# A pre-activation block with table lookups on one Trainium2 core: the order of loads, warm-up products and weight differences at the start of two of its layers

## The chip, the core and the metric

The kernel runs on one core of a Trainium2 chip. The metric is device microseconds of one execution; the time of a kernel is the median of its runs. A core has engines that each work off an instruction queue of their own, in order: TensorE (PE, matrix products; PEld is its weight load), VectorE (DVE), ScalarE (ACT), GpSimd (POOL) and SyncE (SP), which issues most of the transfers. An engine waits on semaphores for what other engines and transfers produce.

## The reference, cut to what matters

Everything is float32. The input has 32 images of 1024 channels, 14 x 14 positions.

```python
def _amm(patches, centroids, lut, inv_temp):       # approximate product by lookup
    v = patches.reshape(B, ncb, sub, H * W).transpose(0, 3, 1, 2)
    scores = 2.0 * einsum('blcs,cks->blck', v, centroids) - sum(centroids * centroids, -1)
    attn = softmax(scores * inv_temp, axis=-1)     # over the 16 centroids of a codebook
    out = einsum('blck,cko->blo', attn, lut)
...
out = _amm(gn(x), c1_centroids, c1_lut, c1_invt)                 # 1024 -> 256, sub 4
out = relu(_bn(out, bn1_g, bn1_b))
out = _amm(_extract3x3(out), c2_centroids, c2_lut, c2_invt)      # 3x3 patches, sub 9
out = relu(_bn(out, bn2_g, bn2_b))
out = _bn(_amm(out, c3_centroids, c3_lut, c3_invt), bn3_g, bn3_b)
x = x + relu(out + gn(x))
x = x + linear_attention_block(gn(x))
```

gn normalises each image in 32 groups of channels; _bn uses mean and variance over all images. The last line is a linear attention with rotary tables and a depthwise 3x3 product; the change doesn't touch it.

## The kernel before, in words

The kernel goes through four stages one after the other: layer 1 (the first lookup product with its group normalisation), layer 2 (the 3x3 one), layer 3, and a last stage with the attention. Each of layers 1 and 2 is worked in 128 **units**: 16 pairs of images (392 positions) by 8 tables of weights. Unit u uses pair u // 8 and table u % 8. A second pass with exact maxima is compiled too and entered only if a check on the sums asks for it; it isn't executed here.

What happens to a unit, with the engine and the lines:

- **Score**: PE multiplies the normalised images with the prepared centroids into four PSUM buffers (L910 in layer 1, L1051 in layer 2). ACT takes exponentials of them into a tile t (L576).
- **Softmax**: DVE transposes t so that the 16 centroids lie side by side (L588), POOL adds halves (L591, from unit 2 on), DVE sums (L607), takes reciprocals (L609) and transposes them back, repeated (L619, tile r), ACT adds up totals for the check (L630), POOL multiplies t by r (L626).
- **Rows**: The 16th centroid's share is one minus the rest, so its row of t is free and used to carry another sub-table's data. For that POOL writes one of every four units' slices to a spare (L621) and SP issues transfers from the spare into the free rows of t (L725, L728).
- **Lookup**: PE multiplies t with the table, 12 or 16 products (L748).

The loop `units` (L732) writes these out by hand, in this order for each i: score and exponentials of unit i + 4, transposition of i + 3, softmax and rows of i + 2 (or i + 3 for the first units), then `side(i)` (L838 in layer 1, `side2`, L1062, in layer 2), which carries whatever has been put at step i, then the lookup of unit i (units 0, 1 and 2 are looked up at i = -2, 0 and 1). Each engine's queue has its instructions in the order in which they are written, so where a piece is written decides what stands behind it. `at(i, piece)` (L806) puts a piece at step i; pieces meant for before the loop come at -5.

A table of weights has to be prepared before its lookup. `packed_lut` (L679) returns the pieces for it, by which the diff indexes: [1] **own** (L687) loads it from memory, [2] **less** (L694) takes the difference to the 16th centroid's entry, [3] **keep** (L703, tables 0 and 4 only) stores a slice to memory, [4] **others** (L706) loads rows from what was kept. A difference is, for each of two halves, one product with a constant matrix on PE (L700) and a copy on ACT (L701):

```python
def less():
    for h in range(2):
        t = weights[b][:, 512 * h : 512 * h + 512]
        ps = scores(512) if b > 3 else None
        if ps is None:
            ps = ps_po.tile([P, 512], F32, tag="po", name="less")
        nc.tensor.matmul(ps, less_last, t, start=True, stop=True)
        nc.scalar.copy(t, ps)
```

The constant matrix `less_last` is made by DVE from an identity matrix (`last_masks`, L673 to L677), with `kmask`, which is made from the identity too (`kmasks`, L215). The identity and three other constants are loaded through ACT's queue at the start (L181). `warm` (L567) multiplies by the identity without using the result.

Layer 1's start, L872 to L902: SP loads the first pair of images (`load_x`, L237), tables 0 and 1, the second pair, tables 2 to 7. DVE makes masks, centroid matrices (L346 to L392) and the statistics of the first pair (L264). The pieces of a group normalisation (`gn_pieces`, L246) are four statistics pieces on DVE, two averages over groups on PE (L274) with DVE between (L282 to L288), and a power and a product on POOL (L295, L296); ACT then normalises channel by channel (L825). For the second pair (x_1) these pieces are put at steps -3 to 2. The scores' bias is a product with a reduction (L401 to L410).

Layer 2's start, L1018 to L1040: ACT normalises the first channels of layer 1's output into a padded tile (L990, `store_pair`, L988), SP stores it to memory (L1002), and 3x3 patches are loaded from there, six transfers to a patch (`load_patches`, L1006, L1012). There are four patch buffers. With `engines=both` transfers alternate by row offset between SP and ACT. `second_half` (L1032) does the same for the other half of the channels.

The last stage isn't written out by hand: a planner (`Plan`, L51) takes pieces with engine, rank, cost and dependences and writes them by simulated due times (L83). It goes round a Python set of engines (L90, L117).

Of the kernel before, what the change touches and what calls it, by code (L numbers as in the profile page):

```python
# [20 lines left out]
HW = 196  # L21
# [128 lines left out]
def conv_preact_kernel(ctx: ExitStack, tc: tile.TileContext, a: dict, out: bass.AP):  # L150
    nc = tc.nc
# [59 lines left out]
    def masks():  # L211
        nc.vector.tensor_reduce(mask8, mask1.rearrange("p (j c) -> p c j", c=8), AX.X, ALU.add)
        nc.vector.tensor_reduce(mask4, mask1.rearrange("p (j c) -> p j c", c=8), AX.X, ALU.add)

    def kmasks():  # L215
        nc.vector.tensor_reduce(kmask, ident.rearrange("p (c k) -> p k c", k=KC), AX.X, ALU.add)
# [290 lines left out]
    def layers(exact, early=None):  # L507
# [59 lines left out]
        def warm(n, rhs):  # L567

            t = scores(rhs.shape[1])
            for _ in range(n):  # L570
                nc.tensor.matmul(t, ident, rhs, start=True, stop=True)
# [222 lines left out]
        with ExitStack() as s:  # L794
# [5 lines left out]
            AHEAD = 2 if exact else 4  # L800
# [50 lines left out]
            luts2 = [packed_lut(2, b) for b in range(8)]  # L851
# [3 lines left out]
                    at(8 * p + c - AHEAD - 1 - (p == 0), normalise(p, c))  # L855
            at(24, edges)
            at(40, masks2)
            for b, i in enumerate((-4, -4, -3, -3, -1, 1, 2, 3)):
                for k in (2, 3, 4):
                    if k != 3 or b % 4 == 0:  # L860
                        at(i, lambda b=b, k=k: luts[b][k]())
# [8 lines left out]

            luts = [packed_lut(1, b) for b in range(8)]
            xts[0] = load_x(xp, 0)  # L872
            for b in range(2):
                luts[b][1]()
            xts[1] = load_x(kept, 1)
            for b in range(2, 8):
                luts[b][1]()
            if not exact:
                masks()
            bias1, biases = score_biases(ps_tr, once, st, 1, raw[1], P, CT, mask8, 4)  # L880
            w1 = score_matrices(once, 1, "", raw[1], mask8)
            gn = [
# [89 lines left out]
        with ExitStack() as s:  # L972
# [4 lines left out]
            NPB = 4  # L977
# [50 lines left out]
            luts2[3][2]()  # L1028
            load_patches(2)
            load_patches(3)  # L1030

            def second_half():  # L1032
                for b in range(4):
                    luts2[b][4](nc.scalar)
                store_pair(0, 1)
                if not exact:
                    load_patches(NPB)

            if exact:
                second_half()  # L1040
            w9, bias2 = parts[2]

            def score2(u):
# [17 lines left out]

            def side2(i):  # L1062

                if i == 1 - ahead and not exact:
                    second_half()
# [47 lines left out]
        with ExitStack() as s:  # L1113
# [8 lines left out]
            luts = luts3  # L1122
# [1176 lines left out]
```

## Time and profile before

| | us |
|---|---|
| three runs | 3385.02, 3385.55, 3385.81; median 3385.55 |
| the profiled execution | 3385.66 |
| its span | 3383.0 |
| layer 1: first score (L910) | 20.11 |
| layer 1: lookups 0, 1, 2, 3 begin (L748) | 33.58, 43.88, 53.11, 65.59 |
| layer 1: lookups 4, 5, 6, 7 begin | 71.83, 77.31, 83.62, 90.43 |
| layer 2: first score (L1051) | 840.07 |
| layer 2: lookups 0, 1, 2, 3 begin | 855.87, 866.85, 877.71, 888.45 |
| layer 2: lookups 4, 5, 6, 7 begin | 894.79, 899.81, 906.15, 912.48 |

The last stage begins at about 2284. TensorE's granted clock over the execution was 0.994 of full speed. In the profile's rows a group is written as tile written <- tiles read, with the number of instructions; "idle before" is how long the engine had stood still and what it was released by. A queue with a q (SPq, ACTq) is an engine issuing transfers.

### The profile page before, as it was taken

What the parts mean: (1) busy time and instruction counts of PE and PEld (TensorE: products, weight loads), DVE (VectorE), ACT (ScalarE), POOL (GpSimd) and SP (SyncE); (2) the same over time, 40 slices, a digit from 0 to 9 for tenths busy, and PEclk for the clock granted to TensorE, in tenths of its full rate; (3) what the DMA queues carried; (4) which work ended last, traced back from release to release, by engine and by line L of the source; (5) the groups of instructions that cost most, each with busy time, mean ns of one, the idle gap of its engine ahead of it and who ended that gap; (6) DMA issues with size and microseconds to landing.
All of it is one profiled execution on the core that took longest, in us unless ns stands there. A gap on an engine that the chain in (4) does not pass through costs nothing. (4 is left out here: it accounts for less than half of the span.)

```text
span 3383.0 us, 61034 instructions
## 1 busy us (share of the span) xinstructions
PE 3300.1 (98%) x22287; PEld 2012.1 (59%) x22287; DVE 2872.0 (85%) x4174; ACT 1789.7 (53%) x4419; POOL 2528.3 (75%) x1562
## 2 busy tenths in 40 slices
PE   8999999999999999999999999989999999999998
PEld 4555555554445544444478888876666666666665
DVE  8999999996888898888666666655899999989996
ACT  5555555553444444444311111108888888888885
POOL 5999999996788889888532222216988888898887
PEclk9999999999999999999999999999999999999999
DMA  3110111003444344443231111113222333233221
GB/s 120 46 49 28 47 46 47 27 27 86 133 124 125 112 121 122 123 112 104 63 89 40 50 50 50 49 48 127 70 83 84 89 93 93 83 94 97 72 87 39
DMA packets 242250, 266.31 MB, mean 79 GB/s; under 512 B 32812, under 2 KB 239700, under 8 KB 241944
## 3 DMA queue, kind: packets, MB, share of 16 engines
q1 hardware_dynamic: 240400, 261.20, 26.3%
q8 instruction: 179, 2.93, 0.4%
q10 hardware_dynamic: 1544, 1.13, 0.1%
q14 instruction: 127, 1.04, 0.1%
HBM read 171.01 MB, written 75.58 MB: 73 GB/s over the span
## 5 line engine op out<-in xcount | busy, mean ns | idle before, releaser
L626 POOL TENSOR_TENSOR t<-t,r 128x1568 f32<-128x1568 f32 (+5 forms) x292 | 962.0, 3296 | 531.5 <-issue 222.8
L748 PE MATMUL po<-t,lut 128*128 128x392 f32 x3840 | 1331.1, 499 | 8.0 <-DMA t<-spare 8.0
L748 PEld LDWEIGHTS po<-t,lut 128*128 128x128 f32 x3840 | 710.1, 190 | 606.1 <-issue 83.3
L1806 PE MATMUL mm<-y,lut 128*128 128x392 f32 x2048 | 713.5, 494 | 6.1 <-ACT vt L1871 4.1
L588 DVE STREAM_TRANSPOSE tt<-t 128x1568 f32<-128x1568 f32 (+1 forms) x284 | 517.5, 1822 | 158.9 <-ACT t L576 155.9
L576 ACT ACTIVATE t<-sc,cbias 128x392 f32<-128x392 f32 (+1 forms) x624 | 322.4, 597 | 560.0 <-PE sc L910 189.6
L2030 DVE SCALAR_TENSOR_TENSOR pa<-y,lepe_w,pa 128x406 f32<-128x406 f32 x900 | 533.5, 635 | 22.2 <-PE pa L2012 20.0
L619 DVE STREAM_TRANSPOSE r<-rc 128x1568 f32<-128x1568 f32 (+1 forms) x284 | 520.8, 1834 | 11.6 <-POOL t L626 1.2
L1806 PEld LDWEIGHTS mm<-y,lut 128*128 128x128 f32 x2048 | 370.0, 188 | 249.6 <-ACT vt L1871 5.0
L591 POOL TENSOR_TENSOR tt<-tt 128x784 f32<-128x784 f32 x252 | 463.4, 1839 | 15.0 <-DVE tt L588 14.9
L576 ACT ACTIVATE t<-sc,room 128x392 f32<-128x392 f32 x512 | 259.1, 589 | 390.9 <-issue 156.8
L1388 PE MATMUL po<-t,lut 128*128 128x224 f32 (+2 forms) x1352 | 313.3, 414 | 0.0
L607 DVE TENSOR_REDUCE sm<-tt 128x98 f32<-128x784 f32 (+2 forms) x284 | 297.0, 1046 | 1.2 <-POOL tt L591 0.8
L1388 PEld LDWEIGHTS po<-t,lut 128*128 128x128 f32 (+1 forms) x1352 | 233.4, 189 | 62.9 <-issue 60.6
L609 DVE RECIPROCAL rc<-sm 128x98 f32<-128x98 f32 (+1 forms) x284 | 220.1, 775 | 9.8
L630 ACT ACTIVATE sm<-sm 128x98 f32<-128x98 f32 (+1 forms) x284 | 85.2, 300 | 154.5 <-DVE rc L609 154.5
L1659 ACT ACTIVATE w<-x,tb,gn_a 128x196 f32<-128x196 f32 x248 | 128.3, 517 | 39.9 <-POOL y L1541 28.1
L1992 POOL TENSOR_TENSOR qr<-qr,zb 128x784 f32<-128x784 f32 x64 | 118.1, 1855 | 28.6 <-DMA zb<-zd 25.7
L1818 ACT ACTIVATE e<-e 128x392 f32<-128x392 f32 x256 | 134.4, 525 | 1.4
L1772 ACT ACTIVATE y<-x,gb,ga 128x196 f32<-128x196 f32 x256 | 122.8, 542 | 14.4 <-POOL gb L1735 14.2
L825 ACT ACTIVATE x<-x,gn_b,gn_a 128x196 f32<-128x196 f32 x256 | 127.5, 557 | 4.8 <-POOL gn_b L296 4.3
L1401 DVE TENSOR_TENSOR o<-po,o 128x224 f32<-128x224 f32 (+1 forms) x156 | 81.5, 543 | 56.8 <-PE po L1388 51.9
(215 smaller groups left out, 4516.7 us busy)
## 6 DMA issues: line engine op xcount, KB each, us to landing
patch<-h1d SPq DMA_DIRECT2D x382, 108.5 KB
x<-in_x_dram SPq DMA_DIRECT2D x32, 784.0 KB
o3d<-o SPq DMA_DIRECT2D x56, 448.0 KB
x<-in_x_dram SPq DMA_DIRECT2D x64, 392.0 KB
out_dram<-x SPq DMA_DIRECT2D x64, 392.0 KB
o<-o3d SPq DMA_DIRECT2D x62, 392.0 KB
h1d<-pad SPq DMA_DIRECT2D x96, 225.0 KB
patch<-h1d SPq DMA_DIRECT2D x382, 54.2 KB
```

Source lines behind the costliest of these rows:

```text
L576: nc.scalar.activation(t[:, j, : sc.shape[1]], sc, AF.Identity if exact else AF.Exp, bias=bias[:, j : j + 1],)
L588: nc.vector.transpose(tt, tf)
L591: nc.gpsimd.tensor_tensor(tv[:, :, :8], tv[:, :, :8], tv[:, :, 8:], ALU.add)
L607: nc.vector.tensor_reduce(sm, tv, AX.X, ALU.add)
L609: nc.vector.reciprocal(rc, sm)
L619: nc.vector.transpose(r, bc(rc, 2, KC))
L626: nc.gpsimd.tensor_tensor(v[:, c], v[:, c], r[:, c], ALU.mult)
L748: nc.tensor.matmul(po[h], luts[b][:, j, h * P : (h + 1) * P], ts[u % len(ts)][:, j, :N2], start=(b == 0 and j == j0), stop=(b == 7 and j = ...
L1388: nc.tensor.matmul(dst, w, x, start=start, stop=stop)
L1806: nc.tensor.matmul(pv(), w[kt][:, m0 : m0 + P], ywin(p, first + kt), start=(kt == 0), stop=(kt == 3),)
L1818: nc.scalar.activation(e(), e(), AF.Exp, scale=-1.0)
L2030: nc.vector.scalar_tensor_tensor(acc, neighbours(p, c, offset(k)), lw[:, c, k : k + 1], acc, ALU.mult, ALU.add,)
```

## The change

In layer 1:

- SP loads all eight tables before the second pair of images.
- `kmasks` and `last_masks` are written before the bias and the centroid matrices, where kmasks was behind the statistics and last_masks behind the bias.
- The warm-up of 9 products has 4, the second warm-up (4 products) is gone.
- The differences of tables 0 and 1 stand behind the warm-up, that of table 2 behind the bias product. Tables 3 and 4 follow the first score, 5 and 6 the second, 7 the third (before: 0 and 1, 2 and 3 behind the first two scores, then 4 at i = -1 and 5, 6, 7 at 1, 2, 3).
- The pieces of x_1's normalisation stand at -1, -1, 0, 0, 1, 1, 2, 2, 2 in place of -3, -3, -2, -1, 0, 0, 1, 1, 2.

In layer 2:

- ACT issues its share of patch 0 alone (by row offsets 2 of its 6 transfers). Patch 1's share, the load of table 7 (4 transfers) and the rows of tables 0 to 3 are issued by SP.
- Before the loop only tables 0 and 1 have their difference; 2, 3 and 4 come at i = -4, -3, -1 and 5, 6, 7 at 4, 5, 6 (before: 0 to 3 before the loop, 4 to 7 at -3, -1, 1, 2).
- The rows (others) of table 0 stand behind patch 3, of 1 at -3, of 2 and 3 at -2, of 4 at 1, of 5, 6, 7 at 4, 5, 6 together with the difference. The load of table 7 stands at -1.

The diff, without what concerns the exact pass alone:

```diff
@@ layer 1 @@
-            for b, i in enumerate((-4, -4, -3, -3, -1, 1, 2, 3)):
+            for b, i in ((3, -4), (4, -4), (5, -3), (6, -3), (7, -2)):
                 for k in (2, 3, 4):
                     if k != 3 or b % 4 == 0:
                         at(i, lambda b=b, k=k: luts[b][k]())
...
             xts[0] = load_x(xp, 0)
-            for b in range(2):
+            for b in range(8):
                 luts[b][1]()
             xts[1] = load_x(kept, 1)
-            for b in range(2, 8):
-                luts[b][1]()
             if not exact:
                 masks()
+                kmasks()
+            last_masks()
             bias1, biases = score_biases(ps_tr, once, st, 1, raw[1], P, CT, mask8, 4)
             w1 = score_matrices(once, 1, "", raw[1], mask8)
...
-            warm(9, xts[0][:, 0, :HW])
-            for k, f in enumerate(gn[0]):
+            warm(4, xts[0][:, 0, :HW])
+            luts[0][2]()
+            luts[0][3]()
+            luts[1][2]()
+            for f in gn[0]:
                 f()
-                if k == 3 and not exact:
-                    kmasks()
             ts = unit_tiles(AHEAD + 2)
             biases()
-            last_masks()
-            warm(4, xts[0][:, 1, :HW])
+            luts[2][2]()
+            for b in range(3):
+                luts[b][4]()
...
             for k, f in enumerate(gn[1]):
-                at((-3, -3, -2, -1, 0, 0, 1, 1, 2)[k] if AHEAD > 2 else k - 7, f)
+                at((-1, -1, 0, 0, 1, 1, 2, 2, 2)[k] if AHEAD > 2 else k - 7, f)
@@ layer 2 @@
-            both = nc.sync, nc.scalar
             store_pair(0, 0)
             luts2[0][2]()
+            load_patches(0, engines=(nc.sync, nc.scalar))
             luts2[1][2]()
-            load_patches(0, engines=both)
-            load_patches(1, engines=both)
-            luts2[7][1](nc.scalar)
+            load_patches(1)
             luts2[0][3]()
-            luts2[2][2]()
-            luts2[3][2]()
             load_patches(2)
             load_patches(3)
+            luts2[0][4]()

             def second_half():
-                for b in range(4):
-                    luts2[b][4](nc.scalar)
+                luts2[1][4]()
                 store_pair(0, 1)
-                if not exact:
-                    load_patches(NPB)
+                load_patches(NPB)
...
             def side2(i):
-                if i == 1 - ahead and not exact:
-                    second_half()
-                if i == 2 - ahead and not exact:
-                    load_patches(NPB + 1)
-                for b in range(4, 8):
-                    if i == (max(b - 7, -ahead) if exact else (-3, -1, 1, 2)[b - 4]):
-                        luts2[b][2]()
-                    if i == max(b - 4, 0):
-                        luts2[b][4]()
-                if i == max(-2, -ahead):
-                    luts2[4][3]()
+                if exact:
+                    ...
+                else:
+                    if i == -3:
+                        second_half()
+                    if i == -2:
+                        luts2[2][4]()
+                        luts2[3][4]()
+                        load_patches(NPB + 1)
+                    if i == -1:
+                        luts2[7][1]()
+                    b = {-4: 2, -3: 3, -1: 4, 4: 5, 5: 6, 6: 7}.get(i, 0)
+                    if b:
                         luts2[b][2]()
+                    if b == 4:
+                        luts2[b][3]()
+                    if b > 4 or i == 1:
+                        luts2[b or 4][4]()
```

More of the change, by code (lines that the diff above doesn't have):

```diff
@@ L1017, in load_patches @@
                         )
-            both = nc.sync, nc.scalar
             store_pair(0, 0)
             luts2[0][2]()
+            load_patches(0, engines=(nc.sync, nc.scalar))
             luts2[1][2]()
-            load_patches(0, engines=both)
-            load_patches(1, engines=both)
-            luts2[7][1](nc.scalar)
+            load_patches(1)
             luts2[0][3]()
-            luts2[2][2]()
-            luts2[3][2]()
             load_patches(2)
             load_patches(3)
+            luts2[0][4]()
             def second_half():
-                for b in range(4):
-                    luts2[b][4](nc.scalar)
+                luts2[1][4]()
                 store_pair(0, 1)
-                if not exact:
-                    load_patches(NPB)
+                load_patches(NPB)
             if exact:
-                second_half()
+                for b in (2, 3):
+                    luts2[b][2]()
+                    luts2[b][4]()
+                luts2[1][4]()
+                luts2[7][1]()
+                store_pair(0, 1)
             w9, bias2 = parts[2]
@@ L1062, in side2 @@
             def side2(i):
-                if i == 1 - ahead and not exact:
-                    second_half()
-                if i == 2 - ahead and not exact:
-                    load_patches(NPB + 1)
-                for b in range(4, 8):
-                    if i == (max(b - 7, -ahead) if exact else (-3, -1, 1, 2)[b - 4]):
+                if exact:
+                    for b in range(4, 8):
+                        if i == max(b - 7, -ahead):
+                            luts2[b][2]()
+                        if i == max(b - 4, 0):
+                            luts2[b][4]()
+                    if i == max(-2, -ahead):
+                        luts2[4][3]()
+                else:
[6 more added lines that the diff above has]
+                    if i == -1:
+                        luts2[7][1]()
+                    b = {-4: 2, -3: 3, -1: 4, 4: 5, 5: 6, 6: 7}.get(i, 0)
+                    if b:
                         luts2[b][2]()
-                    if i == max(b - 4, 0):
-                        luts2[b][4]()
-                if i == max(-2, -ahead):
-                    luts2[4][3]()
+                    if b == 4:
+                        luts2[b][3]()
+                    if b > 4 or i == 1:
+                        luts2[b or 4][4]()
                 p = {4: 1}.get(i + ahead, (i + ahead + 9) / 8)
```

## The prediction

> **What bounds the kernel now.** I read the share of busy time first, then busy time in stretches of 20 us, then the timeline of the two places that the change touches.
>
> The page's engine line:
>
> ```profile
> PE 3300.1 (98%) x22287; PEld 2012.1 (59%) x22287; DVE 2872.0 (85%) x4174; ACT 1789.7 (53%) x4419; POOL 2528.3 (75%) x1562
> ```
>
> TensorE is busy for 98% of the span: little beyond the two starts can be gained. Stretches (columns: length, busy PE, weight load, DVE, ACT, POOL, granted clock, DMA share, GB/s):
>
> ```profile
> 0.00:20.00 20.00, 8.17 (x36) 7.10 (x36) 11.05 (x42) 2.27 (x3) 2.28 (x9) 1.00 0.92 276
> 20.00:40.00 20.00, 16.53 (x64) 6.73 (x63) 17.80 (x26) 15.62 (x35) 8.19 (x7) 1.00 0.38 122
> 40.00:60.00 20.00, 18.84 (x71) 9.29 (x70) 19.23 (x29) 10.25 (x25) 15.76 (x8) 1.00 0.33 97
> 60.00:80.00 20.00, 19.79 (x72) 10.14 (x73) 18.95 (x24) 13.40 (x34) 19.40 (x10) 1.00 0.04 11
> 80.00:100.00 20.00, 20.00 (x79) 10.63 (x78) 17.75 (x21) 10.50 (x27) 17.99 (x8) 1.00 0.20 57
> 840.00:860.00 20.00, 14.62 (x109) 5.03 (x109) 14.05 (x9) 8.97 (x20) 7.49 (x6) 0.69 0.32 95
> 860.00:880.00 20.00, 16.75 (x133) 7.21 (x132) 14.84 (x12) 9.83 (x22) 13.38 (x6) 1.00 0.53 158
> 900.00:920.00 20.00, 20.00 (x148) 10.14 (x148) 17.88 (x14) 8.76 (x22) 18.46 (x9) 1.00 0.49 135
> ```
>
> From 80 us on PE has no gap: whatever lateness it has then is carried to the stage's end. Before that DVE (17.8 to 19.2 of 20) is the fuller engine beside it. Layer 2 starts the same way and PE is full from 900 us. So two delays must be found: how much later lookup 7 (L748) comes in each layer.
>
> The timeline of layer 1's start (start, us, engine, line, count, idle before and releaser):
>
> ```profile
> 2.28 0.60 ACTq L181 DMA_DIRECT2D ident<-in_ident_dram  x1
> 7.04 0.15 DVE L346 TENSOR_SCALAR cinvt1b<-invt 128x1 f32<-128x1 f32 x1 [3.54 <-DMA invt<-in_invt_dram]
> 9.70 4.66 PE L571 MATMUL sc<-x,ident 128*128 128x196 f32 x18 [9.70 <-DMA ident<-in_ident_dram]
> 10.92 4.31 DVE L264 BATCH_NORM_STATS2 gst<-x 128x6 f32<-128x196 f32 x16
> 15.15 0.35 DVE L216 TENSOR_REDUCE kmask<-ident 128x16 f32<-128x128 f32 x1
> 18.80 0.99 ACT L825 ACTIVATE x<-x,gn_b,gn_a 128x196 f32<-128x196 f32 x2 [3.08 <-POOL gn_b L296]
> 23.21 1.81 DVE L588 STREAM_TRANSPOSE tt<-t 128x1568 f32<-128x1568 f32 x1 [1.89 <-ACT t L576]
> ```
>
> DVE is the chain here: matrices 7.04 to 10.92, statistics to 15.2, then the normalisation. What reads ident can't start before 9.7.
>
> The timeline of layer 2's start:
>
> ```profile
> 829.88 3.42 ACTq L1012 DMA_DIRECT2D patch<-h1d  x4
> 833.34 4.00 ACTq L692 DMA_DIRECT2D lut<-in_lut_dram  x4
> 837.43 1.56 ACT L701 COPY lut<-less 128x512 f32<-128x512 f32 x3 [7.61 <-DMA lut<-in_lut_dram]
> 838.07 2.07 PE L700 MATMUL less<-lut,less_last 128*128 128x512 f32 x2 [6.29 <-ACT lut L701]
> 843.88 1.81 DVE L588 STREAM_TRANSPOSE tt<-t 128x1568 f32<-128x1568 f32 x1 [14.76 <-ACT t L576]
> 884.93 1.98 PE L700 MATMUL sc<-lut,less_last 128*128 128x512 f32 x4 [0.84 <-ACT t L576]
> ```
>
> Eight transfers hold ScalarE's queue for 7.4 us; its copies, and so PE's next difference (L700) and the first scores, stand behind them.
>
> **Layer 1, step by step.** (1) kmask and the two masks after it read ident and now head DVE's queue. Before, DVE worked from 7.04 on without ident. Now it sits until 9.67, where PE's first weight load was free to go: kmask .35 plus cblock and less_last .87 (20.44 to 21.31) end at 10.9, the two preparations at L386/L388 at 11.3, the matrices (3.88) at 15.2, the statistics (16 instructions, 4.28) at 19.5 against 15.2: **+4.3**. All of the normalisation behind them moves with it: last statistic gve 17.50 to 21.9, gn_b 18.76 to 23.04. Bound: ident shares ScalarE's queue with invt, which landed at 7.04; were ident there so early, 2.6 of this would go.
>
> (2) PE: nine warm-up products become four, the second warm-up goes. They ran in 9.70 to 14.36 and 18.69 to 20.18, while PE had nothing else to do: gain 0, but for the 0.50 that ACT's second normalisation waited on the last one (20.28). Differences 0 and 1 run in their place from 10.9 to 16, beside the statistics: cost 0.
>
> (3) Difference 2 stands behind the bias product (17.73 to 18.85, now 22.0 to 23.1): 1.98, to 25.0. ACT has its copies ahead of the first normalisation, two at about .55, to 25.55; the normalisation could have begun at 23.08 (gn_b's end): **+2.5**. First score 20.11 to 26.5, first exponential 21.18 to 27.5, first transpose 23.21 to 29.55: **+6.3** (4.3 + 2.5 - 0.5).
>
> (4) What comes back: three differences, 2 us each, leave the stretch after the first score; DVE loses .87 of masks there, and has 2.1 of idle from 24 to 80. But PE isn't the limit: lookup 0 waits for unit 0's softmax (12.4 from exponential to lookup, 21.18 to 33.58) and lands at 40.9 against 33.58. DVE's 54 us of work for units 0 to 7 goes on behind 29.55: r of unit 7 about +4.3. Replaying the engines' orders with the row durations I get lookup 2 at 59.2 (53.11 before), 3 at 67.9 (65.59).
>
> (5) The second images load behind all tables: x_1's two transfers start after about 16.5 instead of 7.07 and land near 26, ahead of its first statistics (29.41 before), so cost 0. But its normalisation's pieces stand one to two units later in the order, on DVE, PE and POOL. Before, POOL's power ended at 66.43, score 8 ran at 70.95 behind lookup 3 and waited for nothing. Now the power ends about 75, score 8 runs at 76, lookup 4 at 77 (71.83): +5.2. Lookups 5, 6, 7 at 82.6, 89, 96 against 77.31, 83.62, 90.43: **layer 1 +5.4**. Without (5)'s new wait about +2.7; least, with ident early too, 0.
>
> [...] Rows first: PE's clock stayed at 1.00 from its stop at 831.8 until about 835 and was 0.62 in the next microsecond, some 3.6 to 4 us of silence. In my replay PE stops at about 16.3 and has the group product at 19.6: 3.3 us, just short. [...] If it falls, the products between 19.6 and 26.5 (.62 + .62 + 1.12 + 1.98 + .9, of which about half lies on the chain) take twice as long: +2.6 at least, and up to +5.2; by the rows I take 0.
>
> **Layer 2, step by step.** (6) ACT keeps only its 2 transfers for patch 0 (.85 each by 3.42/4), so is free at 831.6 instead of 837.34. Patch 0 was on its queues first; its 6 transfers, 4 from SP and 2 from ACT and now not interleaved with patch 1's, are issued by 832.5 (SP took .66 each from 829.87); with the 2.3 us from a row transfer's issue to the lookup that waits for it (875.39 to 877.71) they land near 834.5. Score 0 runs at 835 against 840.07, first transpose 838.6 against 843.88: **-5.3**. DVE's idle of 14.76 shrinks by that. Lookup 0, without the 2.69 us of four table transfers that ACT issued at 848.75, comes at 849.3 against 855.87 (-6.5).
>
> (7) What ACT gave up is issued by SP: 2 transfers of patch 1, 4 of table 7, 4 table rows: about .6 each (3.71 for six in steady state), 6 us in all. SP's order is then the limit: row transfers (L725) of unit 2 stand behind patch transfers, and lookup 2 comes at 874.4 (877.71: -3.3), lookup 4 at 891.9 (894.79: -2.9).
>
> (8) Differences 5, 6 and 7 stood at 863.33, 874.03 and 884.93, in stretches where PE had gaps (3.25 idle in 860 to 880, .84 in the next). Now they come in units 4, 5, 6, behind 891.9, where PE has none. Each costs its 1.98 and a wait of .5 to .8 for a free buffer (884.93 shows .84): 2.6 each, 7.8 together, of which one was already paid at 884.93; net +5.3. Rows of table 5 (L707) now stand on SP behind unit 6's row transfer, which I put at about 2.5 us more for lookup 5 (902.3 against 899.81). Lookup 7: 912.48 to 917.8, **layer 2 +5.3**; without the wait on SP +2.7. If patch 0 lands only at 837, the early gain halves but the end stays near +4.6, since step 8 sets it. Bounds: -2 if the gaps swallow two of the differences, +8 if SP's lateness adds to all.
>
> **Sum.** 5.4 + 5.3 = 10.7; I take +10, because idle of DVE and PE that a replay by hand fixes in place tends to be used. On the profiled execution's 3385.66 (span 3383.0) that is 3395.7; the median shown is 3385.55, so **3395.5 us**. The last stage isn't touched, but its planner goes round a set of engines (L90, L117), so ties can be ordered otherwise in a new build. No row prices it; PE has 33.9 us of gaps in that stage (busy 1065.1 of 1099.0), and I allow that ties add or take a seventh of them, 5 us either way.
>
> **Rivals.** (a) *PE's own work sets the end in both starts.* Then layer 1 gains: first score 6.4 later, less 6.0 of differences gone, less 4.8 of PE's gaps (20 to 80) closed, -4.4; layer 2 -5.3 from step 6. 3376, faster. For it: PE at 16.5 to 19.8 of 20 in these stretches. Against: the gaps end on a softmax or a row transfer, and DVE is as full. It decides if PE's gaps between first score and fullness stay under 4.8 in layer 1 and step 8's differences replace gaps. 0.08.
> (b) *Partial cancelling*: no exposed wait in (5) (+2.7), layer 2 between -1 and +2.7: 3385 to 3391. Same. 0.30.
> (c) *My forecast*, both starts late, 3392.3 to 3400. 0.44.
> (d) *The clock falls in layer 1* (+2.6 to +5.2) or SP adds to all lookups (+8): 3400 to 3407. 0.18.
>
> A measurement tells about 0.2% (6.8 us) from no change: faster below 3378.8, slower above 3392.3. Faster .08, same .30, slower .62. Range 3384 to 3406: it leaves out (a) and a tail of (d).
>
> **What will show it.** In the profile after: kmask as DVE's first wait, on ident, at about 9.7 (step 1; at 7 it was wrong); statistics at 15.2; first normalisation behind copies (step 3); POOL's power for x_1 ending after lookup 3 (step 5); PE's clock in 16 to 20; layer 2's score 0 near 835 (step 6); differences 5 to 7 between lookups 4 and 7 with PE at 20.00 of 20 (step 8). I'm wrong if PE's gaps before 80 and before 900 are fewer by more than the first scores are later, or if the pace per pair in the full part (49.3 and 48.06 us between equal rows) changes.

## The result, and the profile after

The changed kernel takes 3398.83 us (median of 5 runs, 3397.45 to 3406.68) beside 3385.81 us before (5 runs, 3385.02 to 3387.87): a ratio of 1.0041, 95% interval 1.0027 to 1.0056. It is slower, by 13 us where 10 were forecast. The profiled execution took 3397.45 us with a span of 3395.5 us, 12.5 us over the span before.

Where the 12.5 us arose, by the starts of the same instructions in both traces:

| stretch | before | after | difference |
|---|---|---|---|
| layer 1: lookup 7 of the first pair begins | 90.43 | 95.69 | +5.26 |
| layer 1: first output copy of the last pair (L758) | 823.17 | 828.44 | +5.27 |
| layer 2: lookup 7 begins, from that copy | 89.32 | 98.40 | +9.1 |
| layer 2: the rest, from its lookup 7 to its last output copy | 726.6 | 725.5 | -1.1 |
| layer 3 (last output copy of layer 2 to PE's first product of the last stage) | 645.5 | 645.8 | +0.3 |
| last stage, to the end | 1098.4 | 1097.4 | -1.0 |

Both losses lie in the first pair of a layer, as forecast; from there on a lateness is carried unchanged: at each of its first eight pairs layer 2 is exactly 14.36 us late.

The page's engine line of the changed kernel:

```profile
PE 3302.7 (97%) x22269; PEld 2013.5 (59%) x22269; DVE 2870.9 (85%) x4174; ACT 1788.3 (53%) x4419; POOL 2527.9 (74%) x1562
```

PE's busy time grew by 2.6 us, the span by 12.5: what was added is waiting. Stretches of the changed kernel (columns: length, busy PE, weight load, DVE, ACT, POOL, granted clock, DMA share, GB/s):

```profile
20.00:40.00 20.00, 17.42 (x51) 7.20 (x52) 11.59 (x15) 13.95 (x31) 7.15 (x9) 0.91 0.40 123
40.00:60.00 20.00, 19.30 (x61) 9.61 (x60) 18.23 (x28) 10.14 (x24) 13.49 (x7) 0.83 0.32 93
60.00:80.00 20.00, 19.83 (x69) 10.51 (x68) 19.73 (x31) 10.65 (x29) 17.07 (x8) 0.91 0.01 4
80.00:100.00 20.00, 20.00 (x81) 10.75 (x80) 19.73 (x24) 10.37 (x26) 19.92 (x10) 1.00 0.03 10
860.00:880.00 20.00, 10.56 (x118) 4.37 (x116) 15.57 (x12) 8.86 (x20) 14.65 (x7) 0.87 0.50 135
900.00:920.00 20.00, 16.38 (x103) 7.74 (x104) 13.00 (x11) 8.03 (x20) 17.18 (x8) 1.00 0.51 151
```

DVE does 11.59 us of work in the second stretch where it did 17.80: the chain through DVE starts late. PE looks busier in 20 to 60 than before, but at a clock of 0.91 and 0.83 instead of 1.00: products that take longer count as busy (the bias product below took 2.07 us for 1.12). In layer 2, PE has 10.56 of 20 in 860 to 880 (16.75 before), and in 900 to 920, where it had no gap, it has 3.6 us of them.

The timeline of layer 1's start in the changed kernel:

```profile
9.49 0.37 DVE L216 TENSOR_REDUCE kmask<-ident 128x16 f32<-128x128 f32 x1 [6.42 <-DMA ident<-in_ident_dram]
14.83 4.31 DVE L264 BATCH_NORM_STATS2 gst<-x 128x6 f32<-128x196 f32 x16
19.20 0.62 PE L274 MATMUL gn_ps<-gst,gavg 128*128 128x16 f32 x4 [1.90 <-DVE gst L264]
21.64 2.07 PE L401 MATMUL pb<-croom 128*128 128x512 f32 x2 [0.27 <-DVE gve L288]
26.59 1.87 ACT L825 ACTIVATE x<-x,gn_b,gn_a 128x196 f32<-128x196 f32 x4
30.64 1.81 DVE L588 STREAM_TRANSPOSE tt<-t 128x1568 f32<-128x1568 f32 x1 [5.26 <-ACT t L576]
```

DVE sits 6.42 us for the identity; the statistics begin 3.9 us later. The bias product takes 2.07 us where it took 1.12 in the kernel before: the clock, not the work.

```profile
17.73 1.12 PE L401 MATMUL pb<-croom 128*128 128x512 f32 x2 [0.27 <-DVE gve L288]
```

Windows of the changed kernel around that product show it (PE clock is the third column from the end):

```profile
20.00:21.00 1.00, 0.25 (x3) 0.25 (x3) 0.63 (x5) 0.00 (x0) 0.00 (x0) 1.00 1.10 346
21.00:22.00 1.00, 0.73 (x5) 0.64 (x5) 0.17 (x1) 0.00 (x0) 0.34 (x1) 0.73 1.10 337
22.00:23.00 1.00, 1.00 (x2) 0.47 (x2) 0.00 (x0) 0.00 (x0) 0.92 (x3) 0.50 1.11 336
```

From the first score to lookup 7 of layer 1, before and in the changed kernel (columns as in the stretches):

```profile
20.11:90.43 70.32, 65.48 (x250) 31.54 (x249) 65.68 (x89) 42.86 (x101) 53.52 (x27) 1.00 0.21 66
27.63:95.69 68.06, 67.19 (x236) 33.29 (x237) 62.63 (x83) 39.69 (x95) 49.19 (x24) 0.92 0.12 35
```

PE stands still for 0.87 us there, where it stood still for 4.84: once the scores have begun, layer 1 of the changed kernel has hardly a gap on PE, but 10.24 us of it are at half clock. Score 8, the first of the second pair, follows lookup 3 without a wait:

```profile
69.02 7.23 PE L748 MATMUL po<-t,lut 128*128 128x392 f32 x16
76.17 0.94 PE L912 MATMUL sc<-x,cw 32*128 32x392 f32 x8
```

The timeline of layer 2's start, in the changed kernel:

```profile
835.13 2.03 ACTq L1014 DMA_DIRECT2D patch<-h1d  x2
840.61 1.62 PE L1053 MATMUL sc<-patch,room 27*32 27x392 f32 x32 [6.15 <-DMA patch<-h1d]
865.08 8.26 SPq L1014 DMA_DIRECT2D patch<-h1d  x12
873.39 2.00 SPq L692 DMA_DIRECT2D lut<-in_lut_dram  x4
879.79 0.62 SPq L725 DMA_DIRECT2D t<-spare  x1
882.16 6.93 PE L748 MATMUL po<-t,lut 128*128 128x392 f32 x16 [9.62 <-DMA t<-spare]
900.33 1.98 PE L700 MATMUL sc<-lut,less_last 128*128 128x512 f32 x4 [0.83 <-ACT t L576]
```

ScalarE's two transfers are gone by 837.2, and the first score comes 12.2 us after layer 1's copy instead of 16.9. Then PE waits 9.62 us in front of lookup 2 for one row transfer, which SP issued at 879.79, behind twelve patch transfers, table 7 and six more. Before, that wait was 1.69 us:

```profile
877.71 5.50 PE L748 MATMUL po<-t,lut 128*128 128x392 f32 x16 [1.69 <-DMA t<-spare]
```

From the first score to lookup 7 PE stands still for 22.21 us in the changed layer 2, for 9.47 before. The difference at 900.33 stands in front of lookup 4.

### The profile page after: what moved, and what is told of

It is laid out like the page before. It is cut to its first block, busy times and chain, and to the rows that moved or that the text cites. A ratio compares the mean times of both kernels' runs of the same rounds, so it can differ in the third digit from the quotient of the medians.

```text
span 3395.5 us, 60997 instructions
## 1 busy us (share of the span) xinstructions
PE 3302.7 (97%) x22269; PEld 2013.5 (59%) x22269; DVE 2870.9 (85%) x4174; ACT 1788.3 (53%) x4419; POOL 2527.9 (74%) x1562
## 5 line engine op out<-in xcount | busy, mean ns | idle before, releaser
L1053 PE MATMUL sc<-patch,room 27*32 27x392 f32 x4096 | 123.1, 502 | 8.2 <-DMA patch<-h1d 7.4
```

## The experiments

In all of them the planner goes round its engines in a fixed order, by this edit:

```diff
-        engines = {p[0] for p in self.pieces}
+        engines = sorted({p[0] for p in self.pieces}, key=str, reverse=True)
```

With `reverse=True` (order B) all four engines' instructions of the last stage stand in the same order as in the profiles of before and after; without it (order A) they don't. Only kernels of one order can be set beside each other as whole times. Within a layer the starts from the profile serve: layer 1 from the span's start, layer 2 from layer 1's first output copy of the last pair. All profiles:

| kernel | edits of layer 1 | PE clock 15 to 97 us | first score | lookup 4 | lookup 7 | edits of layer 2 | first score | lookup 2 | lookup 3 | lookup 7 | last stage |
|---|---|---|---|---|---|---|---|---|---|---|---|
| before | none | 1.00 | 20.11 | 71.83 | 90.43 | none | 16.90 | 54.54 | 65.28 | 89.32 | 1098.4 |
| c1_before_order_b | none | 0.96 | 21.77 | 75.21 | 93.81 | none | 17.19 | 55.23 | 65.97 | 90.00 | 1097.8 |
| a2_layer2 | none | 0.96 | 21.68 | 75.10 | 93.70 | all | 12.05 | 53.41 | 65.66 | 99.54 | 1098.5 |
| d3_less_act | none | 0.98 | 20.14 | 73.55 | 92.16 | step 6 alone | 11.85 | 51.98 | 64.42 | 88.45 | 1079.5 |
| after | all | 0.92 | 27.63 | 77.05 | 95.69 | all | 12.18 | 53.72 | 64.66 | 98.40 | 1097.4 |
| a1_layer1 | all | 0.90 | 27.91 | 80.69 | 99.30 | none | 17.44 | 55.81 | 66.55 | 90.58 | 1096.7 |
| c2_after_order_a | all | 0.92 | 28.72 | 78.08 | 97.11 | all | 11.79 | 53.23 | 65.18 | 98.23 | 1079.9 |
| a4_rows_act | all | 0.92 | 28.57 | 77.96 | 96.98 | rows 1 to 3 by ACT | 11.70 | 51.63 | 64.87 | 107.63 | 1097.9 |
| c3_diffs_early | all | 0.92 | 28.81 | 78.25 | 97.27 | early differences | 12.11 | 53.16 | 65.60 | 97.89 | 1079.9 |
| c4_rows_first | all | 0.88 | 28.89 | 81.68 | 100.28 | rows before patches | 12.10 | 49.69 | 61.79 | 101.20 | 1078.9 |
| a3_masks | masks later | 0.92 | 24.75 | 75.84 | 94.44 | all | 11.76 | 55.09 | 67.19 | 100.75 | 1098.0 |
| d1_early_both | x_1's pieces early | 0.92 | 27.71 | 77.66 | 96.26 | early differences and rows | 11.98 | 53.51 | 67.29 | 91.32 | 1080.7 |
| d2_rows_by_act | 9 warm-up products | 0.88 | 29.07 | 81.83 | 100.44 | table rows by ACT | 11.74 | 52.75 | 64.84 | 99.09 | 1079.5 |
| d4_both_layers | masks later, difference 2 and those after it later, x_1's pieces early | 0.98 | 22.06 | 71.02 | 90.05 | step 6 alone | 11.86 | 53.33 | 65.49 | 89.52 | 1079.5 |

### One layer's edits alone: a1_layer1, a2_layer2

The edits of the change that concern the other layer are taken back.

> Only the edits of layer 1; layer 2 is written as before. In this and all further kernels the planner goes round its engines in a fixed order, the one that both traces show, so that the last stage can't differ by ties. My theory (the two layers add up, each through its own lookup 7): lookup 7 of layer 1 at 95.7 us as in the changed kernel (90.43 before), layer 2 then as before but 5.3 later, span 3383.0 + 5.3 = 3388.3, the ratio to the kernel before 1.0016. Rival (most of the 12.5 us of span comes from layer 2 and what follows, and layer 2 takes layer 1's lateness up): span below 3385.

> Only the edits of layer 2. In the changed kernel layer 2's first pair ended 9.09 us later than layer 1's lateness explains, and 1.07 came back later in the layer. My theory: that is this layer's own, so lookup 7 of layer 2 at 912.48 + 9.1 = 921.6, span 3383.0 + 8.0 = 3391, ratio 1.0024. Rival (the 9.1 hangs on where the clock's dips fell after layer 1's shift): lookup 7 at 917.8, as in my prediction, span near 3387.

Measured: a1_layer1 3392.33 us (3387.88 to 3396.91), span 3390.4; a2_layer2 3397.42 us (3391.89 to 3397.91), span 3395.9. Their order B is that of c1_before_order_b (3387.99, in a later comparison), by which layer 1's edits cost 1.0013 and layer 2's 1.0028. That comparison ran on another chip, and set against the kernel before of each comparison the two come to 1.0006 and 1.0016, so whole times don't size the shares; the starts have to. Both theories hold as to place: layer 2 with its code as before ends within 1.3 us of before (a1: 90.58), and layer 2's edits cost their 9 us and more beside an unchanged layer 1 (99.54), so they don't hang on layer 1's shift. How much of them is the clock's isn't told apart by this, for it fell at nearly the same place (875.15 to 885.39 in a2, 874.79 to 885.03 in the changed kernel). But both spans are longer than expected, by 2.1 and 4.9 us: in a1 lookup 7 of layer 1 came at 99.30 and not at 95.7, and in a2 3.3 of it is layer 1 with the code of before, 93.70 for 90.43. The column of PE's clock goes with it.

### The masks: a3_masks

```diff
             if not exact:
                 masks()
-                kmasks()
-            last_masks()
             ...
             w1 = score_matrices(once, 1, "", raw[1], mask8)
+            if not exact:
+                kmasks()
+            last_masks()
```

> The changed kernel with kmask and the two masks behind the centroid matrices instead of ahead of them, so that DVE doesn't begin with a wait for the identity; all else as changed. My theory (step 1 sets the start, through the chain statistics, normalisation, first score): statistics begin at 10.92 + 1.2 = 12.2 instead of 14.83, PE's gap before the group product goes from 1.90 to nothing and with it the half clock at 21.5 to 24.9, first score at 23.5 to 24.5 instead of 27.63, lookup 7 at 92 to 93 instead of 95.69, span -3. Rival (x_1's normalisation, now late in the order, holds lookup 4 whatever the start does): first score earlier as well, but lookup 7 stays at 95 or later, span within 1 of the changed kernel's 3395.5.

Measured: 3397.81 us (3396.40 to 3399.28), span 3397.4. The first score comes at 24.75, 2.9 to 4.1 us earlier than in the kernels with the change's layer 1, close to the 23.5 to 24.5 expected. Lookup 7 at 94.44 is 1.3 to 2.8 us earlier than in the five other profiles with a clock of 0.92. So step 1 is confirmed in kind, and lookup 4 does follow the start, against the rival; but about half of what the start wins is lost again on the way to lookup 7, where PE stands still for 2.54 us instead of 0.87. The gap before the group product went, as expected, but not the half clock: the clock was at 0.50 from 19.85 to 23.26, and in three more windows. So in this run the clock fell without that gap. The whole time shows nothing of the gain: this run's layer 2 was 2.3 us slower than the changed kernel's.

### The rows by ACT: a4_rows_act

```diff
-                    spare_rows(ts, u)
+                    spare_rows(ts, u, nc.scalar if u < rows else nc.sync)   # rows = 4 in layer 2
```

> The changed kernel with the row transfers of units 1, 2 and 3 of layer 2 issued by ACT instead of SP, one edit in layer 2. In the changed kernel unit 2's share was multiplied by 872.45, but SP issued its row at 879.79, behind 18 patch transfers, table 7 and two tables' rows, and lookup 2 waited for it until 882.16. Theory (SP's queue is what took back step 6's gain): lookup 2 at about 875 to 876, lookup 3 at 886 instead of 893.09, lookup 7 some 5 to 7 us earlier than 926.84, span 3389 to 3391. Rival (the late differences 5 to 7 set the end and SP's lateness is hidden behind them): lookup 2 as early, but lookup 7 less than 2 us earlier, span above 3393.5.

Measured: 3410.65 us (3407.63 to 3413.26), lookup 2 at 51.63, lookup 7 at 107.63. This edit doesn't tell the theories apart, for it brought waits of its own. Waits of SP in this kernel, 846 to 900 us (instruction, waited for, total, times, longest):

```profile
SPq L1004 <- DMA t<-spare: 6.6, 1, 6.6
SPq L1014 <- DMA t<-spare: 4.5, 1, 4.5
```

By the profile's releasers, SP's stores and patches wait for the landing of rows that ACT issues; ACT issues them only when POOL's product is there (861.33 for unit 1). Score 4 then waited 7.04 us for its patch. The changed kernel has no such waits: what was moved to the other queue here wasn't free of the first.

### The planner's order: c1_before_order_b, c2_after_order_a

No edit but the order above; c2_after_order_a is the changed kernel without `reverse=True`.

> The kernel before with one edit: the planner of the last stage goes round its engines in the fixed order that the profiled before and the changed kernel both show (order B). In the last comparison the kernel before ran at 3369.97, 15.6 us under its time of 3385.55 beside the changed kernel. Theory (that build had the planner's other order, and the order of ties is worth 15 us): this kernel at 3385, ratio 1.0045. Rival (another chip, or another day, is that much faster for all): this kernel at 3370, ratio 1.000.

> The changed kernel with the planner's other order (order A), whole change in place. Theory (the change costs its 13 us in layers 1 and 2 whatever the last stage's order): 3383, ratio to the kernel before 1.0039 if that has order A, and the last stage some 15 us shorter than the 1097.4 us of the changed kernel. Rival (the two interact): ratio under 1.002.

Measured: c1_before_order_b 3387.99 us beside 3367.68 of the kernel before, ratio 1.0059 (1.0044 to 1.0075); c2_after_order_a 3383.30 us, ratio 1.0047 (1.0033 to 1.0061), its last stage 1079.9 instead of 1097.4 us. Both theories hold: the order in which a set hands out four engines is worth 18 us in the last stage, more than the whole change, and the change costs the same in either order. The build of the kernel before in these comparisons wasn't profiled; that it had order A is inferred from its time.

### Layer 2, differences and table rows: c3_diffs_early, d1_early_both, d2_rows_by_act

```diff
c3_diffs_early, d1_early_both
-                    b = {-4: 2, -3: 3, -1: 4, 4: 5, 5: 6, 6: 7}.get(i, 0)
+                    b = {-4: 2, -3: 3, -1: 4, 0: 5, 1: 6, 2: 7}.get(i, 0)
d1_early_both also: rows of tables 4 to 7 at i = 1, 2, 3, 4
+                    k = {1: 4, 2: 5, 3: 6, 4: 7}.get(i, 0)
d1_early_both also, layer 1
-                at((-1, -1, 0, 0, 1, 1, 2, 2, 2)[k] if AHEAD > 2 else k - 7, f)
+                at((-3, -3, -2, -1, 0, 0, 1, 1, 2)[k] if AHEAD > 2 else k - 7, f)
d2_rows_by_act
-                        luts2[b or 4][4]()
+                        luts2[b or 4][4](nc.scalar if b > 4 else nc.sync)
d2_rows_by_act also, layer 1
-            warm(4, xts[0][:, 0, :HW])
+            warm(9, xts[0][:, 0, :HW])
```

> The changed kernel in order A, with the differences of tables 5, 6 and 7 of layer 2 at steps 0, 1 and 2 instead of 4, 5 and 6; their rows stay where the change put them. In the changed kernel, counted from layer 1's last output copy but one (828.44), lookup 3 comes at 64.65 and lookup 7 at 98.40, 33.75 apart; before they are 24.03 apart. Theory (step 8: each late difference costs 2.7 on PE because PE has no gap there): lookups 3 to 7 24 to 25 us apart, lookup 3 up to 3 later, lookup 7 at 91 to 93, 6 us off the time. Rival (SP's lateness or the clock set that stretch): lookup 7 not under 96.

> The changed kernel, order A, with one edit in each layer, read from the profile apart. Layer 2: the differences of tables 5 to 7 at 0, 1, 2 and their rows at 2, 3, 4 instead of with the differences at 4, 5, 6, where in the kernel with early differences alone lookups 5 and 6 stood 10.9 and 8.7 behind their forerunner. Theory (rows behind a unit's row transfer on SP hold lookups 5 and 6 as much as the differences do, so that either alone changes nothing): lookups 3 to 7 24 to 26 us apart (33.75 with the change, 32.29 with early differences alone), lookup 7 at 89 to 91 from layer 1's first output copy (98.2 to 99.5). Rival (SP's total load): still over 30 apart. Layer 1: x_1's normalisation pieces where they stood before. Theory (step 5, the late power): lookup 4 no longer waits for it, lookup 7 at 94.5 to 95 instead of 95.7 to 97.3 (six profiles of the changed layer 1 gave 95.69 to 100.28). Rival: unchanged, 97 or more.

> The changed kernel, order A, with one edit in each layer. Layer 2: differences 5 to 7 stay late, but their rows are issued by ACT, right behind ACT's own copies of them, so that they stand behind nothing on SP. Theory (late differences cost PE 2.7 each by themselves): lookups 3 to 7 31 to 33 us apart, lookup 7 at 96 to 98. Rival (only the rows' place on SP): 25 to 27 apart, lookup 7 at 91. Layer 1: nine warm-up products again instead of four. Theory (the clock's fall at 19.5 to 22 comes from PE's gap before the group product, which nine products fill by putting off the first two differences): bias product back at 1.12 from 2.07 us, difference 2 at 1.98 from 2.56, first score at 26.5 instead of 27.6 to 28.9. Rival (the clock falls because small products leave PE idle from 19 to 21.5, gap or not): first score 27.6 or later.

Measured, lookups 3 to 7 apart: 33.05 to 33.88 with the change, 32.29 in c3, 34.25 in d2, 24.03 in d1; before 24.04. The theory of c3 failed: with early differences alone lookup 7 came at 97.89, not at 91 to 93. What stood in the way, in c3_diffs_early:

```profile
909.71 3.50 POOL L626 TENSOR_TENSOR t<-t,r 128x1568 f32<-128x1568 f32 x1
910.04 0.62 SPq L725 DMA_DIRECT2D t<-spare  x1
910.70 0.58 SPq L707 DMA_DIRECT2D lut<-tables  x1
912.88 7.88 PE L748 MATMUL po<-t,lut 128*128 128x392 f32 x16 [5.84 <-issue]
```

Lookup 5 begins 2.18 us after the issue of table 5's rows, which stand on SP behind a unit's row transfer and the patches before it. The line names no releaser, but unit 2's row in the changed kernel took as long from issue to lookup (879.79 to 882.16), and with these rows early too (d1) the wait is gone. With early differences their 7.8 us (three times 2.6) go, but PE's wait for these rows grows from 1.63 to 5.84 us, and lookup 5 falls into half clock (910.86 to 917.69) and takes 7.88 us for 5.53: 8.2 of the 8.3 us that c3 has more than before.

With the rows taken out of SP's way instead (d2), the differences hold by themselves: three times 2.6 to 2.7 us on PE, though SP now waits 11.7 us with patches and 3.4 us with a store for rows that ACT issued. The other 2.1 of the 10.2 us that d2 has more than before are lookup 3 at half clock (7.04 us for 5.53) and 0.6 us of wait for a row transfer. Only with both early (d1) are the lookups as close as before. So the late place of a difference and the late place of its rows, which must stand behind it, each cost about 8 us over these lookups, the rows' with the clock's help, and hide behind each other. d1 took 3373.86 us, 1.0017 (1.0008 to 1.0026) of the kernel before, against 1.0047 for the changed kernel in the same order: 9.4 us come back, of which 6.9 in layer 2's lookup 7.

The two edits in layer 1 both failed to help. With x_1's pieces at their old places (d1) lookup 4 is at 77.66 and lookup 7 at 96.26: no gain. POOL's power for x_1 began at 71.00 instead of 71.79: it stands behind unit 4's product on POOL (68.37 to 71.07) in either order. Nor was there a wait to gain: in the changed kernel too, PE goes from lookup 3 into score 8 (76.17) without a gap. With nine warm-up products (d2) the first score came at 29.07, the bias product still took 2.07 us, and the clock fell for two windows, 20.45 to 27.27, though PE's stop before the group product was 1.00 us instead of 1.90.

### SP's order: c4_rows_first

```diff
-                        luts2[7][1]()
+                        luts2[7][1](nc.scalar)
+                    if 2 < i + 4 < 9:
+                        load_patches(i + 4 + NPB - 1)      # was in score2, ahead of the row transfer
```

> The changed kernel in order A, with two edits that relieve SP's queue at layer 2's start and leave PE's order as it is: the load of table 7 is issued by ACT, and for units 3 to 8 the next patch is issued behind the unit's row transfer instead of ahead of it. Issuing the rows from ACT had made layer 2 9 us later, because ACT then stood waiting for POOL's product ahead of its exponentials; here nothing on ACT waits. Theory (SP's queue holds lookups 2 and 3): counted from 828.44 in the changed kernel, lookup 2 at 46 to 49 instead of 53.72, lookup 7 at 92 to 94 instead of 98.40. Rival (the late differences alone): lookup 7 at 96 or later.

Measured: 3382.06 us, ratio 1.0044 (1.0028 to 1.0059); lookup 2 at 49.69 and lookup 3 at 61.79, both some 3 to 4 earlier than in the change, but lookup 7 at 101.20. SP's queue does hold lookup 2, as the theory has it; freeing it there didn't reach lookup 7, which the late differences and rows hold (10.3, 12.1 and 10.7 us between lookups 3, 4, 5 and 6). The rival is nearer.

### What is worth keeping: d3_less_act, d4_both_layers

```diff
d3_less_act, on the kernel before
-            load_patches(1, engines=both)
-            luts2[7][1](nc.scalar)
+            load_patches(1)
 ...
+                if i == -1:
+                    luts2[7][1](nc.scalar)
d4_both_layers, the same, and in the change's layer 1 (with the edits of a3 and d1)
-            for b, i in ((3, -4), (4, -4), (5, -3), (6, -3), (7, -2)):
+            for b, i in ((2, -4), (3, -4), (4, -3), (5, -3), (6, -2), (7, -1)):
-            luts[2][2]()
```

> The kernel before, order A, with step 6 alone: ACT issues its share of patch 0 only, SP that of patch 1, and ACT loads table 7 four steps later; differences and rows stand where they stood. Theory (step 6 is a gain of 5 us at the first score, lost in the changed kernel to SP's added work and the late differences and rows): first score of layer 2 at 12 from layer 1's first output copy (16.9 to 17.4 before), lookup 7 at 85 to 87 (89.3 to 90.6), 3 to 4 us faster than the kernel before, ratio 0.999. Rival (SP's queue takes it back here too, at unit 2's row): lookup 2 at 53 or later and lookup 7 not under 89.

> Layer 2 as in the run before this one. Layer 1 as changed (tables first, four warm-up products, first two differences beside the statistics), but with the masks behind the centroid matrices, difference 2 behind the first score, one difference later each after it, and x_1's pieces where they stood before: steps 1, 3 and 5 undone, the rest of the change kept. Theory (those three steps are the loss of layer 1): first score at 21 to 23, lookup 7 at 90 to 92 (90.4 to 93.8 before, 95.7 to 100.3 changed), 3 to 6 us faster than the kernel before together with layer 2's gain. Rival (the differences now stand too late for DVE's pace, or the clock falls in the gap without warm-up): lookup 7 at 94 or later, no gain beyond that of the run before this one.

Measured: d3_less_act 3366.25 us (11 runs), ratio 0.9996 (0.9987 to 1.0005); d4_both_layers 3368.32 us (11 runs), ratio 1.0001 (0.9992 to 1.0010). Neither can be told from the kernel before in order A (3367.75, 27 runs). In d3 the first score is 5 us earlier, lookup 2 2.6 to 3.8 earlier than in the three profiles with the layer as before, lookup 7 only 0.9 to 2.1: the expected 85 to 87 isn't reached. SP waits in d3, 826 to 935 us:

```profile
SPq L1012 <- DMA lut<-tables: 3.8, 1, 3.8
SPq L1012 <- DMA h1d<-pad: 2.6, 3, 1.3
SPq L1012 <- DMA lut<-in_lut_dram: 2.5, 2, 1.6
```

SP's patches wait here for table transfers that ACT issued (3.8 + 2.5). In d4, layer 1 did as its theory said, first score 22.06 and lookup 7 at 90.05, the earliest of all profiles, with one window at half clock; since it undoes three steps at once, it doesn't say which of them counts. But layer 2 was no better than before (89.52) and its other runs don't show the gain. No version beats the kernel before but by the planner's order: before in order A (3367.75) is some 18 to 20 us under order B (3385.81 and 3387.99).

## Why the prediction was right, and where it wasn't

**Layer 1 (forecast +5.4, measured +5.26).** The row-by-row times came out close: statistics 15.2 (14.83), gve 21.9 (21.41), first normalisation 25.55 (26.59), first score 26.5 (27.63), lookup 0 40.9 (41.37), 2 59.2 (59.64), 3 67.9 (69.02), 4 77 (77.05), 7 96 (95.69). Steps 1 and 3 stand for the first score: a3 took back part of step 1, d4 both, with the first score at 22.06. Behind the first score the agreement is in good part luck: a wait that I priced isn't there, and the clock, which I priced at 0, is in its place.

- *Step 5.* Its new wait, worth 2.7 of the 5.4 us, isn't there. ACT had normalised x_1's first channels by 76.03, and score 8 began at 76.17 right behind lookup 3, PE without a gap. That is the forecast 76, but because lookup 3 began 3.4 us late and needed 7.15 us up to score 8, in half clock from 69.24, where it had needed 5.36. Score 8's lateness is these two, 3.4 and 1.8 us.
- *The clock's bill.* I took 0 for a fall of the clock, since PE's longest stop, 3.3 us in my replay, lay just under the 3.6 to 4 us of the row I read (by the profile 3.46: PE stopped at 831.78, the clock fell at 835.24). That was one stop, and no run shows an edge in a stop's length: in the changed kernel PE stopped for 1.90 us, and the clock fell to 0.50 all the same, from 21.46 to 24.87; the bias product and difference 2 took 1.5 us longer by it. It fell again at 48.76 and 69.24. The layer's 5.26 us add up so: the first score 7.52 later, PE's gaps from there to lookup 7 3.97 less, its work at full clock 3.41 less (three differences), and 10.24 us at half clock, 5.12 us lost. These 5.12 can't simply be taken off again: c2, c3 and a4 lost 3.41 us to the clock there and had gaps of 2.9 us. The eight profiles with the change's layer 1 (two of them with an edit that changed nothing) have lookup 7 at 95.69 to 97.27 with a clock of 0.92 and at 99.30 to 100.44 with 0.90 and 0.88; the four of before's layer 1 at 90.43 (1.00), 92.16 (0.98) and 93.70 to 93.81 (0.96). Both sets rise by 3.3 to 3.7 us for 0.04 of clock, and 0.04 of 82 us is 3.3. By that slope most of layer 1's loss is the clock's; this is argued from the set, not shown, since no run kept the clock up in the change's order. My rival (d) came true in its cause without its size.
- *Step 4.* I wrote that PE isn't the limit. Behind the first score it nearly was, with 0.87 us of gaps in 68.06.

The before I set my sums against was also the best case of its kind: its layer 1 had no window at half clock, others of the same code had one or two.

**Layer 2 (forecast +5.3, measured +9.1 at lookup 7 and +8.0 at the layer's end).** Step 6 was right: first score 4.7 earlier (forecast 5.3), lookup 0 6.4 (6.5). The mis-sized term is what step 7 leaves of it: lookup 2 0.8 earlier, not 3.3. I had SP as the limit, with 6 us of added transfers, but not that it has no pause from unit 1's row at 863.06 to unit 2's at 879.79: eighteen patch transfers, table 7, rows of two tables and a stored slice, while unit 2's product was ready at 872.45. That is 2.5 of the 3.8 us by which lookup 7 missed the forecast; the other 1.3 arise behind lookup 2, which at half clock took 6.93 for 5.50. Step 8 was right in size (lookups 2 to 7 43.4 apart forecast, 44.7 measured, 34.8 before), and its wait on SP, for which I put 2.5 us, was 1.63. But the first of its differences stands in front of lookup 4, not behind it, the sign I named, PE at 20.00 of 20, failed (16.38 in 900 to 920), and I hadn't seen that the late rows alone would cost as much as the late differences.

**The rest.** -1.1 in layer 2 near 1206 to 1304, where layer 3's matrices are made, and -1.0 in the last stage aren't explained. Taking +10 for a sum of 10.7 went the wrong way: the profiled executions are 11.8 us apart, the spans 12.5. The last stage's ties, for which I allowed 5 us, are worth 18; the two kernels compared had the same order, so the allowance wasn't called on, and a build with the other would have put the forecast far out.

**The rivals.** (a), that PE's own work sets the end in both starts, failed in layer 2, where PE's gaps grew. In layer 1 its mechanism came nearer than mine, since the gaps behind the first score were closed (4.84 to 0.87 us); its gain didn't come because of the clock and a first score later than it allowed. (b), a partial cancelling, supposed no exposed wait in step 5. That came true, but the clock took its place in the time, and layer 2's +9.1 lay far outside what (b) allowed.

## What to carry to other kernels

Before moving transfers from one issuing queue to another, write out that queue's whole order up to the first consumer and look for the row that stands last in it; a transfer that is early on the list can cost a later, smaller one more than it gained. Work taken out of a busy start into a stretch without gaps had to be paid in full here (2.6 to 2.7 us for each of three differences in d2_rows_by_act), and what had to follow it, a table's rows, was late with it, so that undoing one of the two showed nothing: test them together. Before blaming code for a few us, profile the unchanged code more than once: the clock's windows moved the same layer by 3 us (lookup 7 at 90.43 and 93.81 from the same code of layer 1), and an unordered set in a planner by 18.

## What the runs showed of the hardware that I had not expected

In the profiles of before and after the granted clock is 1.00 or 0.50 and nothing between, and between its first and its last change each stretch at one level lasts 3.41 us or a whole multiple of it (in the changed kernel 3.41 at 0.50 from 21.46, 23.89 at 1.00 from 24.87, 6.83 at 0.50 from 48.76); a window is one such step. They lay differently in the two: the first fall came at 835.24 in the kernel before, at 21.46 in the changed kernel. A fall came here without a long stop: in the changed kernel the clock fell after the window 18.04 to 21.46, in which PE was busy 36% of the time by the profile, in small products, and at 69.24 after a window of 95% with no stop over 0.17 us, with score products on 32 rows among its work. And a longer stop didn't always bring one: in the changed kernel it stayed up after the window 24.87 to 28.28, with 54% and a stop of 1.56 us. Nor did it follow PE's busy share alone: in the kernel before it stayed up after a window of 59% (29.69 to 33.10). What decides a fall, no run here shows.

Transfers of the two issuing queues weren't independent in these runs: by the profile's releasers, SP waited 6.6 and 4.5 us (a4_rows_act) and 11.7 and 3.4 us (d2_rows_by_act) for the landing of transfers that ACT had issued, into other tiles than those it was about to load. In the kernel before, SP waited so for 7.1 us on table rows from ACT, and the change's own profile has no such wait. Whether the queues or semaphores of the program ask for it, no run here shows.
